# Window attention of a four-layer stack: VectorE in the loop's order, the routing in fixed slots, exponentials behind copies, weights loaded first

## The chip, the cores and the metric

The kernel runs on one core of a Trainium2 chip. A core has five engines with a queue of instructions each: TensorE (PE: matmuls and weight loads, PEld), VectorE (DVE), ScalarE (ACT), GpSimd (POOL) and SyncE (SP), which here only issues DMAs. The metric is the device time of one execution in microseconds (us). Before the change the median of three runs is 2851.44 us (2844.81 to 2851.49). One further execution was taken by the hardware profiler.

## The reference

Four layers over a batch of 2 images with 256 channels and 32 x 32 positions, in float32. Layers 0 and 1 are attention over the feature map. Their result is read as 2 x 1024 tokens of 256 values, and the layer that concerns us is the third, layer 2:

```
t = t + window_attention(layernorm(t))        # windows of 64 tokens, shifted by 32, 8 heads of 32
t = t + moe2(layernorm(t))                    # 8 experts, top 2 of a softmax router, GELU, 256 -> 1024 -> 256

window_attention(x):  q, k, v = x @ w_qkv.T + b_qkv
                      sim = q k / sqrt(32) + rel_pos[i - j]; masked in the last window; softmax
                      out = (softmax @ v) @ w_out.T + b_out
moe2(x):              p = softmax(x @ Wr + br); weights of the top two, normalised to sum 1
                      h = gelu((layernorm(x) * ln_g[e] + ln_b[e]) @ W1[e] + b1[e])
                      y = h @ W2[e] + b2[e]; weighted sum of the two experts' y
```

The factors ln_g and ln_b are each expert's own. Layer 3 is an additive attention (tanh of q_i + k_j for every pair of tokens of an image) and a second mixture of 8 experts with hidden size 512.

## The kernel before

The tokens lie in `t`, 16 tiles of 128 tokens; tiles 0 to 7 are image 0, 8 to 15 image 1. `window_attention` (line 778) works a tile a slot: 16 slots and 4 more to drain. In slot i, TensorE is given `value(i)` (ps_va), `scores(i)` (ps_s), `turn(i-2)` (transposes of the probabilities, ps_pt), one part of the next group's q and k (`project`, ps_qk), `sums(i-3)` (ps_av) and `output(i-4)` (ps_wo). Five of these take a tile of the pool ps_mm, which has three buffers; ps_s and ps_av have one each. `normed(b)` makes the normalised and transposed tokens of image b; for image 1 it is taken in pieces in slots 0 to 5.

Within the loop, TensorE and ScalarE follow the order in which the program writes the instructions (`manual_schedule` with these two engines). For VectorE, GpSimd and SP a planner fixes the order when the kernel is built: it takes from the instructions that are ready by its own reckoning the one that was written first. On ScalarE the exponential of slot i (L884) is written before the two copies of the turned probabilities of tile i-2 (L909). The score work of a slot on VectorE is L876 (scale and add the position bias), L882 (row maximum), L883 (subtract), then after the exponential L885 (sum) and L886 (reciprocal); the division is a product on GpSimd (L889, two instructions). The output of a tile goes through VectorE (L935: y = ps_wo + b_out) and GpSimd (L936: t = t + y).

The routing of image 0 (`dispatch(2, 0)`) is a generator: each `next` issues one piece. It is a gate for each half of the image (statistics L1087 and L1088, inverse root L1072 to L1079, norm L1097, transposes ps_tr L1108 with copies L1109, router L1137, logits L1141), the `route` (top two, counts over all tokens, prefix sums, slot numbers, tiles' experts, affine rows; L1205 to L1313), a second norm of the normalised tokens, and for each of the 8 token tiles two scatters by GpSimd (L1161) into the DRAM buffer `slots_in`; `shift` then adds the mixture of the experts' b2 to t (ps_wT L1179, ps_b L1187, L1189). From slot 10 on the loop takes three pieces a slot; what is left is step D20 of the plan that follows.

That plan (`Late.run`, line 1704) merges generators by due times: E20 are the experts of image 0 (23 slot tiles of 128 rows: `inputs` loads xr by SP, `turn` ps_x, `up` ps_h, `down` ps_y), D21 the dispatch of image 1, E21 its experts, C20 and C21 gather and add the results, A0 and A1 are layer 3's additive attention, and so on. What is due before E21 (172) is ordered by the planner on every engine; after that TensorE, ScalarE and VectorE follow the merge. Expert weights are gathered by GpSimd (`fetch`, L1322) into tiles `ew`, which lie in a pool opened only after window attention, as does kT of layer 3. SBUF is a stack of pools: a new pool's first writers wait for the last reader of the pools that lay there.

The constructor of `Late` loads small constants of layers 2 and 3 (SP and ScalarE queues); `window_attention` then loads its own weights behind them, at L793 to L796.

Of the kernel before, what the change touches and what calls it, by code (L numbers as in the profile page):

```python
# [69 lines left out]
class Stack:  # L70
# [707 lines left out]
    def window_attention(self, t, late):  # L778
# [7 lines left out]
        with ExitStack() as ctx:  # L786
# [6 lines left out]
            w_qkv = self.load(w, "w_qkv", "(c p) o -> p c o", p=P)  # L793
            w_out = self.load(w, "wa_w_out", "(c p) o -> p c o", p=P)
            b_qk = self.load(w, "b_qk")
            b_v, b_out = self.load_row(w, "b_v"), self.load_row(w, "wa_b_out")  # L796
# [25 lines left out]
            uT, q, k, v, pT, o = {}, {}, {}, {}, {}, {}  # L822
# [22 lines left out]
            def project(g, part):  # L845
# [11 lines left out]
                if part < CC:  # L857
                    nc.scalar.activation(to, ps, AF.Identity, bias=b_qk[:, part : part + 1])
                else:
                    nc.vector.tensor_scalar(to, ps, b_qk[:, part : part + 1], None, ALU.add)  # L860

            def scores(i):
# [21 lines left out]
                nc.scalar.activation(l, l, AF.Exp)  # L884
# [8 lines left out]
            def value(i):  # L893
# [7 lines left out]
                nc.vector.tensor_tensor(v[i], ps, b_v, ALU.add)  # L901
# [25 lines left out]
            def output(i):  # L927
                x = o.pop(i)
                ps = late.misc([P, C], "ps_wo")
                for c in range(CC):  # L930
                    nc.tensor.matmul(
                        ps, lhsT=x[:, c, :], rhs=w_out[:, c, :], start=(c == 0), stop=(c == CC - 1)
                    )
                y = sb.tile([P, C], F32, name="y")
                nc.vector.tensor_tensor(y, ps, b_out, ALU.add)  # L935
                nc.gpsimd.tensor_tensor(t[:, i, :], t[:, i, :], y, ALU.add)  # L936
# [5 lines left out]
            with tc.manual_schedule(engines={engines.PE, engines.Activation}):  # L942
                for part in range(2 * CC):
                    project(0, part)
                for i in range(NT + 4):
# [3 lines left out]
                    if 2 <= i < NT + 2:  # L949
                        turn(i - 2)  # L950
                    if i + 4 < NT:
                        project(i // 4 + 1, i % 4)
                    if i < 6:
                        next(other, None)
                    if 3 <= i < NT + 3:
                        sums(i - 3)
                    if 4 <= i:
                        output(i - 4)
                    if i >= 10:
                        for _ in range(3):  # L960
                            next(route, None)
# [28 lines left out]
class Late:  # L990
# [3 lines left out]
    def __init__(self, ctx, stack, t):  # L994
# [4 lines left out]
        self.early = ctx.enter_context(tc.tile_pool(name="early_sb", bufs=2))  # L999
        self.made = {}  # L1000
# [3 lines left out]
        tl = lambda name, shape: self.w.tile(shape, F32, name=name)  # L1004
        self.wr = {l: stack.load(self.w, n, "(c p) e -> p c e", p=P) for l, n in ((2, "wr"), (3, "gate_w"))}
# [87 lines left out]
    def scale(self, dst, src, tiles, mv):  # L1093
        nc = self.nc
        rs = self.inverse_root(mv[:, :, 1], 1e-5)
        for k, i in enumerate(tiles):
# [47 lines left out]
    def dispatch(self, *key, done=0):  # L1144
# [3 lines left out]
        n = len(tokens)  # L1148
        for half in range(done, n // 4):
            yield from self.gate(l, b, half)  # L1150
        yield from self.route(key, n)
        u = self.u[key]
        if l == 2:
            yield from self.norm(lambda i: u[:, i, :], lambda i: u[:, i, :], range(n))
        p, shares, slots, rows = self.routes[key]
        nc = self.nc
# [13 lines left out]
        if l == 2:  # L1170
            yield from self.shift(*key)
# [412 lines left out]
    def project(self, b, half):  # L1584

        nc, U, R = self.nc, 32, 4
        if half == 0:
            self.qb[b] = self.sb.tile([P, IT, U], F32, name="qb")
            self.kT[b] = self.sb.tile([P, N], F32, name="kT")
# [114 lines left out]
    def run(self, route):  # L1704
# [5 lines left out]
        self.loaded = [  # L1710
            [self.sb.tile([P, WIDE], F32, name=f"ew{k}", bufs=LANES[2]) for k in range(2)] for _ in range(LANES[2])
        ]
# [5 lines left out]
            "D21": (self.dispatch(2, 1), (), 5, 3.45),  # L1718
            "E21": (self.experts(2, 1), ("D21", "E20"), 172, lambda now: 2.43 if now < 205 else 4.4),
            "C20": (self.collect(2, 0), ("E20",), 172, 2.0),  # L1720
            "A0": (self.additive(0), ("C20",), 211, 4.75),
            "N30": (self.gate(3, 0, 0), ("A0 half",), 420, 6.0),
            "C21": (self.collect(2, 1), ("E21",), 456, 2.0),
# [113 lines left out]
```

## Time and profile before

| | us |
|---|---|
| median of three runs | 2851.44 |
| the profiled execution, whole | 2887.74 |
| its span, first to last instruction | 2886.0 |
| TensorE busy in the span | 2635.3 (91%) |
| VectorE, ScalarE, GpSimd busy | 1944.8, 1815.6, 1235.5 |
| last product of layer 1 ends | 1623.2 |
| first projection of window attention (ps_qk) | 1640.5 |
| score addition of slots 0, 8, 12 starts | 1650.76, 1702.93, 1735.97 |
| first scatter of image 0 starts | 1779.64 |
| first product of the experts of layer 2 (ps_h) | 1810.79 |

In the profile's lines, L852 is line 852 of the kernel; `ps_qk<-uT,sb_w_qkv` names what an instruction writes and reads. A row of the timeline or of the chain begins with its start and its length in us. The chain is the work that ended last, followed backwards: at each step to what released the instruction, or to the one before it on its engine; "issue" is time for which nothing is recorded. Busy times in a stretch are by engine, with the number of instructions in brackets; a fp32 matmul counts as two records. PEclk is the clock that TensorE was granted, as a share of full speed.

### The profile page before, as it was taken

Reading aid. Unit: us, or ns where it says so; the run is one execution under the profiler, and the core shown is the slowest. Engines: PE = TensorE matmul, PEld = TensorE weight load, DVE = VectorE, ACT = ScalarE, POOL = GpSimd, SP = SyncE. Lnnn points to the kernel's source line nnn. Section 1 sums busy time; section 2 is a strip of 40 time slices with the busy share of each in tenths; the row PEclk is TensorE's granted clock in tenths of the full one; section 3 lists DMA queues with packets and bytes.
Section 4 is the critical chain, followed back from the end, with each engine's and each line's share of the span. In section 5 each row is a group of like instructions: output and inputs, shape, how many; then the busy total and the mean of one; then the engine's idle time right before and its main releaser. Section 6 shows DMA issues by size and latency. Waiting matters only on the chain. (4 is left out here: it accounts for less than half of the span.)

```text
span 2886.0 us, 77396 instructions
## 1 busy us (share of the span) xinstructions
PE 2635.3 (91%) x32006; PEld 1643.6 (57%) x32006; DVE 1944.8 (67%) x3642; ACT 1815.6 (63%) x2685; POOL 1235.5 (43%) x1302
## 2 busy tenths in 40 slices
PE   7899999999999998799999686999999988999987
PEld 3455555555555555555555454998666632465676
DVE  5999999999999999478789577633422343134242
ACT  2777777778777777255555231211699878889722
POOL 4877777777777775001111134244111112102242
PEclk9999999999999999899999897999999999899998
DMA  3000000000000000111010100543222001322354
GB/s 133 3 3 3 3 3 3 3 3 3 3 3 3 3 3 3 49 31 28 11 31 9 28 1 30 202 134 99 68 81 76 16 24 35 128 67 87 116 166 125
DMA packets 180577, 131.39 MB, mean 46 GB/s; under 512 B 130992, under 2 KB 162368, under 8 KB 173056
## 3 DMA queue, kind: packets, MB, share of 16 engines
q0 software_dynamic: 29232, 81.71, 8.5%
q1 hardware_dynamic: 147824, 44.25, 6.8%
q8 instruction: 251, 4.11, 0.6%
q10 hardware_dynamic: 3168, 0.48, 0.1%
q14 instruction: 102, 0.84, 0.1%
HBM read 181.24 MB, written 29.49 MB: 73 GB/s over the span
## 5 line engine op out<-in xcount | busy, mean ns | idle before, releaser
L188 ACT ACTIVATE sc<-sc,sa_shift 128x1024 f32<-128x1024 f32 x512 | 584.5, 1144 | 153.1 <-DMA sa_shift<-sa_min 150.8
L201 DVE STREAM_TRANSPOSE wt<-sc 128x1024 f32<-128x1024 f32 x512 | 601.5, 1207 | 0.2 <-ACT sc L188 0.2
L1622 ACT ACTIVATE th<-kT,qb 128x1024 f32<-128x1024 f32 x512 | 540.4, 1135 | 66.2 <-PE ps_e L1631 40.1
L211 PEld LDWEIGHTS ps_o<-wt,v 128*64 128x64 f32 x8192 | 444.4, 137 | 188.9 <-issue 106.2
L143 PE MATMUL ps_s<-kT,qT 64*32 64x512 f32 x8192 | 527.6, 595 | 18.0 <-ACT sc L153 17.2
L211 PE MATMUL ps_o<-wt,v 128*64 128x128 f32 x8192 | 505.0, 276 | 26.8 <-DVE oT L372 26.7
L166 POOL TENSOR_TENSOR fold<-sc 128x512 f32<-128x512 f32 x256 | 329.2, 1286 | 195.9 <-ACT sc L153 177.0
L168 POOL TENSOR_TENSOR fold<-sc,fold 128x512 f32<-128x512 f32 x256 | 328.4, 1283 | 21.4
L153 ACT COPY sc<-ps_s 128x1024 f32<-128x1024 f32 x256 | 256.0, 1000 | 111.0 <-PE ps_s L143 57.1
L1631 PE MATMUL ps_e<-th,pick 128*32 128x512 f32 x2048 | 305.7, 613 | 20.5 <-ACT th L1622 9.3
L1404 PEld LDWEIGHTS ps_h<-xe,ew 128*128 128x128 f32 x2320 | 278.1, 194 | 63.6 <-issue 39.0
L150 DVE TENSOR_SCALAR_CACHE_REDUCE sc<-ps_s 128x1024 f32<-128x1024 f32 x256 | 304.3, 1189 | 7.1 <-PE ps_s L143 6.6
L1404 PE MATMUL ps_h<-xe,ew 128*128 128x128 f32 x2320 | 295.0, 281 | 13.7 <-issue 5.6
L1424 PE MATMUL ps_y<-ew,h 128*128 128x256 f32 x1160 | 275.6, 387 | 8.2 <-ACT h L1410 5.6
L143 PEld LDWEIGHTS ps_s<-kT,qT 64*32 64x32 f32 x8192 | 134.4, 106 | 230.2 <-issue 163.4
L1424 PEld LDWEIGHTS ps_y<-ew,h 128*128 128x128 f32 x1160 | 215.6, 193 | 66.7 <-issue 23.0
L630 ACT ACTIVATE sc<-sc,l_least 128x1024 f32<-128x1024 f32 x128 | 146.7, 1147 | 125.8 <-DVE sc L617 125.5
L1415 DVE TENSOR_TENSOR hb<-ps_h,ew 128x512 f32<-128x512 f32 x115 | 79.4, 691 | 207.3 <-PE ps_h L1404 167.1
L1428 DVE COPY y<-ps_y 128x256 f32<-128x256 f32 x99 | 41.9, 423 | 229.7 <-PE ps_y L1424 209.9
L1393 ACT ACTIVATE h<-hb 128x512 f32<-128x512 f32 x115 | 71.5, 623 | 193.0 <-DVE hb L1415 173.7
L636 DVE STREAM_TRANSPOSE wt<-sc 128x1024 f32<-128x1024 f32 x128 | 153.3, 1225 | 46.0 <-ACT sc L630 25.4
L617 DVE TENSOR_SCALAR_CACHE_REDUCE sc<-ps_s 128x1024 f32<-128x1024 f32 x128 | 150.7, 1213 | 40.3 <-PE ps_s L609 40.2
(286 smaller groups left out, 3139.1 us busy)
## 6 DMA issues: line engine op xcount, KB each, us to landing
xr<-slots_in SPq DMA_DIRECT2D x99, 128.0 KB
slots_out<-y SPq DMA_DIRECT2D x99, 128.0 KB
sa_got<-sa_least SPq DMA_DIRECT2D x512, 0.5 KB
sa_shift<-sa_min SPq DMA_DIRECT2D x512, 0.2 KB
slots_in<-zero POOLq DMA_DIRECT2D x46, 128.0 KB
kh<-kh SPq DMA_DIRECT2D x32, 128.0 KB
qh<-qh SPq DMA_DIRECT2D x32, 128.0 KB
sa_sums<-sa_total SPq DMA_DIRECT2D x244, 1.0 KB
```

Source lines behind the costliest of these rows:

```text
L143: nc.tensor.matmul(ps[r][S * c : S * (c + 1), a, :].rearrange("p (b i) -> p b i", i=S), lhsT=qT[half, p, S * i : S * (i + 1)], rhs=keys[ha ...
L150: nc.vector.tensor_scalar(scores[m][0], flat[0], 1.0, None, ALU.mult, ALU.min, accum_out=least[m // 2][:, 0, h : h + 1])
L153: nc.scalar.copy(scores[m][1], flat[1])
L166: nc.gpsimd.tensor_tensor(y, a, b, ALU.subtract)
L168: nc.gpsimd.tensor_tensor(y, a, y, ALU.subtract)
L188: nc.scalar.activation(scores[m][r], scores[m][r], AF.Exp, bias=shift[m // 2][:, r : r + 1], scale=-1.0, accum_out=total[i][:, 2 * p + r, ...
L201: nc.vector.transpose(weights[i, h][:, 2 * p + r, :], x)
L211: nc.tensor.matmul(sums[i][64 * k : 64 * (k + 1)], lhsT=v[:, at % NT, 64 * (at // NT) : 64 * (at // NT + 1)], rhs=weights[i, h][:, :, S * ...
L1404: nc.tensor.matmul(ps[:, j, :], lhsT=a[:, c, at : at + P], rhs=x[:, c, :], start=(c == 0), stop=(c == CC - 1),)
L1424: nc.tensor.matmul(ps, lhsT=h[:, j, :], rhs=w2[:, j, :], start=(j == 0), stop=(j == HB - 1))
L1622: nc.scalar.activation(h, keys, AF.Tanh, bias=self.qb[b][:, s // G, g : g + 1])
L1631: nc.tensor.matmul(pe[i][c * U : (c + 1) * U, a, :], lhsT=self.pick[:, k, :], rhs=h[:, a, :], start=(k == 0), stop=(k == G - 1),)
```

## The change

VectorE joins TensorE and ScalarE in following the written order in the loop. The exponential of a slot (`weigh`) is written behind the copies of tile i-2, and the sum, reciprocal and product (`divide`) behind `sums(i-3)`. The k projections are evacuated by ScalarE, as the q ones; v is copied by ScalarE without its bias. Since each row of probabilities sums to 1, b_v adds b_v @ w_out.T to every output: `output_shift` computes it once with TensorE from a widened copy of b_v and adds it to b_out. GpSimd adds b_out to t ahead of time, and VectorE adds ps_wo to t in one instruction.

The routing pieces come by a table of slots (8: 2, 9: 2, 12 to 18: 4, 6, 6, 4, 3, 3, 2; half of each before the slot's output, half behind), 32 in all, which is the whole dispatch of image 0. The second norm no longer takes statistics: its variance is var * rs * rs of the first norm, and its scaling is done by ScalarE, ahead of the route. The first slot tile's expert weights are fetched before the scatters. `shift` of the two images becomes steps B20 (due 100) and B21 (due 215) of the plan. D21 runs the same changed dispatch.

The weights of window attention are loaded first of all by the constructor of `Late`, into a tile `front` whose halves are later kT of layer 3; the expert weight tiles `ew` move from the later pool to the same early pool.

```diff
-            w_qkv = self.load(w, "w_qkv", "(c p) o -> p c o", p=P)
-            w_out = self.load(w, "wa_w_out", "(c p) o -> p c o", p=P)
-            b_qk = self.load(w, "b_qk")
-            b_v, b_out = self.load_row(w, "b_v"), self.load_row(w, "wa_b_out")
+            w_qkv, w_out, b_qk, b_v, b_out = late.windows
...
-            uT, q, k, v, pT, o = {}, {}, {}, {}, {}, {}
+            uT, q, k, v, pT, o, weights = {}, {}, {}, {}, {}, {}, {}
+            spread = w.tile([P, CC, P], F32, name="spread")
+            nc.gpsimd.tensor_copy(spread, broadcast(b_v, [P, CC, P]))
+            def output_shift():
+                ps = late.misc([P, C], "ps_wo")
+                for c in range(CC):
+                    nc.tensor.matmul(
+                        ps, lhsT=spread[:, c, :], rhs=w_out[:, c, :], start=(c == 0), stop=(c == CC - 1)
+                    )
+                nc.vector.tensor_tensor(b_out, b_out, ps, ALU.add)
...
                 to = (q if part < CC else k)[g][:, part % CC, :]
-                if part < CC:
-                    nc.scalar.activation(to, ps, AF.Identity, bias=b_qk[:, part : part + 1])
-                else:
-                    nc.vector.tensor_scalar(to, ps, b_qk[:, part : part + 1], None, ALU.add)
+                nc.scalar.activation(to, ps, AF.Identity, bias=b_qk[:, part : part + 1])
...
                 nc.vector.tensor_tensor(l, l, broadcast(m, [P, H, WIN]), ALU.subtract)
-                nc.scalar.activation(l, l, AF.Exp)
+                weights[i] = l, m, rec
+            def weigh(i):
+                nc.scalar.activation(weights[i][0], weights[i][0], AF.Exp)
+            def divide(i):
+                l, m, rec = weights.pop(i)
                 nc.vector.tensor_reduce(m, l, AX.X, ALU.add)
...
                     )
-                nc.vector.tensor_tensor(v[i], ps, b_v, ALU.add)
+                nc.scalar.copy(v[i], ps)
...
                     )
-                y = sb.tile([P, C], F32, name="y")
-                nc.vector.tensor_tensor(y, ps, b_out, ALU.add)
-                nc.gpsimd.tensor_tensor(t[:, i, :], t[:, i, :], y, ALU.add)
+                nc.vector.tensor_tensor(t[:, i, :], t[:, i, :], ps, ALU.add)
...
             engines = mybir.EngineType
-            with tc.manual_schedule(engines={engines.PE, engines.Activation}):
+            pieces = {8: 2, 9: 2, 12: 4, 13: 6, 14: 6, 15: 4, 16: 3, 17: 3, 18: 2}
+            with tc.manual_schedule(engines={engines.PE, engines.Activation, engines.DVE}):
                 for part in range(2 * CC):
                     project(0, part)
+                output_shift()
                 for i in range(NT + 4):
...
                         turn(i - 2)
+                    if i < NT:
+                        weigh(i)
                     if i + 4 < NT:
...
                         next(other, None)
+                    if 2 <= i < NT + 2:
+                        nc.gpsimd.tensor_tensor(t[:, i - 2, :], t[:, i - 2, :], b_out, ALU.add)
                     if 3 <= i < NT + 3:
                         sums(i - 3)
+                    if i < NT:
+                        divide(i)
+                    for _ in range(pieces.get(i, 0) // 2):
+                        next(route, None)
                     if 4 <= i:
                         output(i - 4)
-                    if i >= 10:
-                        for _ in range(3):
-                            next(route, None)
+                    for _ in range((pieces.get(i, 0) + 1) // 2):
+                        next(route, None)
             return route
...
         self.early = ctx.enter_context(tc.tile_pool(name="early_sb", bufs=2))
+        self.loaded = [
+            [self.w.tile([P, WIDE], F32, name=f"ew{run}{k}") for k in range(2)] for run in range(LANES[2])
+        ]
         self.made = {}
...
         tl = lambda name, shape: self.w.tile(shape, F32, name=name)
+        self.front = self.w.tile([P, 2 * N], F32, name="front")
+        weights = []
+        for name, cols in (("w_qkv", slice(0, 3 * C * CC)), ("wa_w_out", slice(3 * C * CC, 4 * C * CC))):
+            weights.append(self.front[:, cols].rearrange("p (c o) -> p c o", c=CC))
+            nc.sync.dma_start(out=weights[-1], in_=self.ins[name].rearrange("(c p) o -> p c o", p=P))
+        self.windows = (
+            *weights, stack.load(self.w, "b_qk"), stack.load(self.w, "b_v", "(c p) -> p c", p=P),
+            stack.load_row(self.w, "wa_b_out"),
+        )
         self.wr = {l: stack.load(self.w, n, "(c p) e -> p c e", p=P) for l, n in ((2, "wr"), (3, "gate_w"))}
...
         rs = self.inverse_root(mv[:, :, 1], 1e-5)
+        self.last_norm = mv, rs
         for k, i in enumerate(tiles):
...
         n = len(tokens)
+        nc = self.nc
+        again = self.early.tile([P, n], F32, name="again", bufs=1) if l == 2 else None
         for half in range(done, n // 4):
             yield from self.gate(l, b, half)
-        yield from self.route(key, n)
+            if l == 2:
+                mv, rs = self.last_norm
+                to = again[:, 4 * half : 4 * half + 4]
+                nc.vector.tensor_tensor(to, mv[:, :, 1], rs, ALU.mult)
+                nc.vector.tensor_tensor(to, to, rs, ALU.mult)
         u = self.u[key]
         if l == 2:
-            yield from self.norm(lambda i: u[:, i, :], lambda i: u[:, i, :], range(n))
+            rs = self.inverse_root(again, 1e-5)
+            yield 3.0
+            for i in range(n):
+                nc.scalar.activation(u[:, i, :], u[:, i, :], AF.Identity, scale=rs[:, i : i + 1])
+            yield 5.0
+        yield from self.route(key, n)
         p, shares, slots, rows = self.routes[key]
-        nc = self.nc
+        if key == (2, 0):
+            self.fetch(key, 0)
+            self.fetch(key, 0, 1)
...
             yield None if l == 2 else 0.5
-        if l == 2:
-            yield from self.shift(*key)
...
             self.qb[b] = self.sb.tile([P, IT, U], F32, name="qb")
-            self.kT[b] = self.sb.tile([P, N], F32, name="kT")
+            self.kT[b] = self.front[:, b * N : (b + 1) * N]
         cols = slice(half * CH, (half + 1) * CH)
...
         self.p_x, self.p_h, self.p_y, self.p_e = psum("lt_x", 1), psum("lt_h", 2), psum("lt_y", 1), psum("lt_e", 1)
-        self.loaded = [
-            [self.sb.tile([P, WIDE], F32, name=f"ew{k}", bufs=LANES[2]) for k in range(2)] for _ in range(LANES[2])
-        ]
...
             "D21": (self.dispatch(2, 1), (), 5, 3.45),
+            "B20": (self.shift(2, 0), ("D20",), 100, 5.0),
+            "B21": (self.shift(2, 1), ("D21",), 215, 6.0),
             "E21": (self.experts(2, 1), ("D21", "E20"), 172, lambda now: 2.43 if now < 205 else 4.4),
-            "C20": (self.collect(2, 0), ("E20",), 172, 2.0),
+            "C20": (self.collect(2, 0), ("E20", "B20"), 172, 2.0),
             "A0": (self.additive(0), ("C20",), 211, 4.75),
             "N30": (self.gate(3, 0, 0), ("A0 half",), 420, 6.0),
-            "C21": (self.collect(2, 1), ("E21",), 456, 2.0),
+            "C21": (self.collect(2, 1), ("E21", "B21"), 456, 2.0),
             "A1": (self.additive(1), ("C21", "A0 tanh"), 500, 4.6),
...
             "E30": (self.experts(3, 0, then=(3, 1)), ("D30",), 600, 4.4),
```

## The prediction

> **What bounds the kernel now.** I read the page first (TensorE is busy 91% of a 2886.0 us span; most of the rest of its time lies in a few places), then the busy time in stretches around the changed stage, then the chain that ended last inside it, then the rows of each engine. In the stretches the columns are length, then TensorE, its weight loads, VectorE, ScalarE, GpSimd, then the granted clock and DMA.
>
> ```profile
> 1670.00:1690.00 20.00, 17.82 (x220) 11.28 (x216) 12.60 (x27) 6.43 (x14) 7.68 (x8) 1.00 0.01 2
> 1750.00:1770.00 20.00, 11.94 (x135) 8.42 (x133) 18.17 (x64) 3.88 (x9) 5.63 (x6) 0.76 0.00 1
> 1790.00:1810.00 20.00, 11.28 (x32) 7.15 (x33) 8.95 (x34) 0.00 (x0) 15.95 (x18) 0.50 0.42 152
> 1825.00:1850.00 25.00, 25.00 (x180) 23.66 (x179) 12.76 (x35) 5.06 (x7) 7.26 (x8) 1.00 0.14 38
> ```
>
> Window attention (1640 to 1787) is short of TensorE work in every stretch, the gap up to 1810 more so and at half clock; the experts after it are TensorE without a pause. So time saved before 1810.8 moves everything after it, and TensorE work put after it costs its full length. One step of the loop, from the chain:
>
> ```profile
> 1674.91 0.58 ACT ptT L909
> ...
> 1676.77 1.07 PE ps_wo L931 x4
> 1677.86 0.44 DVE y L935
> ...
> 1678.43 0.73 POOL t L936
> 1679.19 0.43 DVE n_st L1087
> ...
> 1680.03 0.59 DVE l L876
> 1680.64 0.70 DVE wa_m L882
> 1681.36 0.70 DVE l L883
> ...
> 1682.68 0.58 ACT ptT L909
> ```
>
> This is a ring of 7.77 us: the copies of turned probabilities wait behind this slot's exponential, that waits for the score work on VectorE, that stands behind a statistic of the route, and that for GpSimd's addition to t of the output that needed the copies. Entry and exit:
>
> ```profile
> 1635.81 4.57 DMA sb_w_qkv<-in_w_qkv
> 1640.51 8.84 PE ps_qk L852 x16
> ...
> 1779.64 1.20 POOL slots_in L1161
> ...
> 1801.60 2.28 DMA slots_in<-u,rt_slot
> 1804.15 4.49 DMA xr<-slots_in
> ...
> 1810.79 1.28 PE ps_h L1404 x6
> ```
>
> The weights are issued last of SP's list, and sixteen scatters start when the slot numbers exist and end 22 us later.
>
> **The skill.** "SBUF — State Buffer" (SBUF: two separate sides) says that VectorE and GpSimd share one pair of ports as an exclusive lock, so that one blocks for the other's whole instruction. The trace agrees: L883 takes 0.70 us alone and 1.58 at 1656.01 beside a GpSimd product. "TensorE: Matmul & The Clock Gate" (Part 1) says that an idle window of about 3.4 us halves the clock; here eight ps_tr took 2.30 us after 4.95 idle, against 1.04. "ScalarE: Activation LUTs" (Table sets) says that identity is in every table set, so the new scalings load none; the existing Identity at L858 stands beside the exponentials without a load.
>
> **The change, part by part** (times of the profiled execution; l(i) is the start of slot i's score addition, L876).
>
> *Entry.* The weights are issued first, at 1623.3, and land by 1627.9 (4.57). TensorE then waits for its own transposes, over at 1634.3, instead of 1640.5. Sixteen projections 8.84, output_shift 1.07 (priced as ps_wo), ps_va 0.86, ps_s 0.42: l(0) at 1645.5. The bias, last of SP's list with one small load more ahead (0.5), was ready at 1644.7 and is now at 1645.2, just in time. Before: 1650.76. **−5.3**. The other small loads come 2 us later for it (four issues of 0.4 to 0.5); the first of them is used in slot 9. Bounds: 0 if the bias is 5 us late, −6.2 if TensorE alone counts.
>
> *Slots 0 to 7.* VectorE per slot: three score instructions 2.13, wait for the exponential 0.65, sum and reciprocal 0.9, addition to t 0.42: 4.1. The bias of v (0.42), the k copies (0.75) and y leave it; on ScalarE: v copy 0.38, two ptT 1.1, exponential 0.63, projection 0.70, oT 0.38, 3.2 in all. TensorE from start to start at full clock: ps_va 0.96, ps_s 0.42, ps_pt 0.95, ps_qk 1.92, ps_av 0.57, ps_wo 0.97: 5.8. TensorE now bounds, with three ps_mm buffers each freed within 1 to 2 us. The exponential now waits behind the copies; behind it stand the q copy and oT, which TensorE needs only in the next slot. Slots 0 to 3 stay VectorE's, since they carry the second image's inverse root (12 small instructions, 0.20 each, 2.4) and eight norms (0.33 each, 2.7): 5.4, 5.7, 3.8, 3.8. Slots 4 and 5 have a transpose each (0.6) but TensorE is about 1 ahead: 11.8. Slots 6 and 7: 11.6. Sum 42.1: l(8) at 1687.6; before 1702.93. **−15.3** so far.
>
> *Slots 8 to 11, first half of the gate.* VectorE in written order can't fill its waits. Slot 8: 3.7 of its own (4.1 less the addition), four statistics 2.2, addition 0.4, root 2.4, four norms 1.4, one port lock 1.0: 11.1. Slot 9: 3.7, two uT copies 1.35, router 1.7, ps_va and ps_s 1.4, and TensorE, idle 3 us, partly at half clock 1.3: 9.5. Slots 10 and 11: 5.8 each and 0.7 for the clock. Sum 32.9: l(12) at 1720.5; before 1735.97. **−15.5**.
>
> *Slots 12 to 14 up to the slot numbers.* Slot 12: 3.7, 2.2, 0.4 (variance of the normed half), 0.4, 2.4, 1.4, then what the trace shows from the second ps_tr at half clock to the next score (1742.87 to 1751.88) 9.0: 19.5. Slot 13: 3.7, 0.4, root 2.4, eight scalings on ScalarE at 0.3 from start to start 2.4 (an estimate from ACT's 128x256 copies, 0.38 with overlap), exponential 0.3, nine small ones 1.9: 11.1. Slot 14: 3.7, 1.2, counts and copies 1.5, prefix 1.9, addition 0.4, eighteen small ones 3.2: 11.9. Locks 2.0. Sum 44.5: slot numbers at 1765.0, before 1779.6. **−14.6**. Bounds: no locks −18; each piece that crosses engines 2 us dearer, eight of them, +1. The second norm's statistics and scalings left VectorE, which is why this equals the old 43.6 without filling.
>
> *GpSimd.* Before, 21.96 from first to last scatter's start with four additions to t among them. Now fifteen intervals of 1.28 (19.2), two fetches 1.31 each, the last products of probabilities 2.15: 24.0, so the last one starts at 1789.0. From there to the first ps_h it was 9.2 (landing 2.3, xr 4.5, transposes and affine): 1798.2. **−12.6**. The bias additions (0.72) are ready slots earlier. The fetches share the software queue, but the last scatter stands 20 us behind them. SP's xr loads are behind nothing new.
>
> *Experts.* Between 1810.8 and 1990.6 TensorE also did D21's router 1.7, ps_tr 1.0, router 1.7, counts 0.5 and shift (two ps_wT 0.6, four ps_b 1.13: 5.7), 10.6 in all, each at full price. Now shift (2,1) leaves and shift (2,0), which lay in the gap, is planned at 100. But the tokens are final at about 1779 (slot 14 needs 3.1 more, slot 15 its 3.7, then product, turn, ps_av and ps_wo about 7), and the gap lasts to 1798; this part of the plan is ordered by readiness (D21's statistics of u ran at 1811.7 though they are emitted after the route), so gates and some of the shift fill the gap at half clock. Bounds 0 and −10.6; I take **−6**. B21 at 215 falls in a stretch where TensorE is at 25.00 of 25 and ScalarE at 23.5 to 25: **+5.7**, bounds 0 and +8. VectorE's relief in D21 and eight scalings on ScalarE are hidden: 12.8 and 5.1 of 25 busy. The new home of ew and kT costs nothing: same lifetimes, fetched earlier.
>
> Sum −12.6 − 6 + 5.7 = **−12.9**: the profiled 2887.74 becomes 2874.8. That execution is 36.3 above the median of 2851.44; I carry the difference over: **2838.5**.
>
> **Rivals.** (1) *The gap takes nothing*: −12.6 + 5.7 = −6.9, 2844.5. For it: ps_wT ran in sequence at 1937, 60 us after p was ready; against it: TensorE was then full, in the gap it isn't. (2) *Scatters behind the last probabilities* on GpSimd, whose order the planner writes: they wait 3.1 for the rest of slot 14, 3.7 of slot 15, then the product; +6.8 on GpSimd's line, so −6.1, 2845.3. Against it: before, additions to t stand between scatters, so ready work goes first. (3) *VectorE's order becomes the ring*: waits in slots 8 to 14 cost 22 more than counted (1750 to 1770 has VectorE at 18.17 of 20 even with filling, and small instructions of 0.8 to 1.0 beside GpSimd instead of 0.2), about 1.1 for each of twenty pieces: +9, 2860. It decides when l(8) to the slot numbers passes 99 us instead of 77 (before: 76.6). Slower. (4) *The weights don't come early*, the memory being freed with all of layer 1: that is already so at 1623.3, and I count only the list's order.
>
> **Chances.** Likeliest 0.57, own range 2826 to 2843; (1) and (2) together 0.23; (3) 0.20. A measurement here can tell 0.3%, 8.6 us, from no change. Faster 0.58 (a little of (1) included), same 0.22, slower 0.20. The range takes in −27 (no locks, whole gap used: −18 + 2 − 10.6, B21 free) and +11: 2824 to 2862.
>
> **What would show it.** First ps_qk near 1634; slots 4 to 7 at 5.8 with TensorE unbroken and ptT ahead of the exponential; VectorE waiting for ps_tr and router in slots 9 and 12; first scatter near 1765, first ps_h near 1798; ps_wT and routers before that ps_h; ps_b again after C20. Wrong if l(8) comes after 1695, if scatters start after 1775, or if TensorE pauses among the experts.

## The result, and the profile after

| kernel | median, us | n | ratio to before, 95% interval |
|---|---|---|---|
| before | 2848.5 | 20 | |
| changed | 2854.38 | 20 | 1.0018 [1.0012, 1.0024] |

The forecast was 2838.5, counted from 2851.44, the median of three runs; twenty runs of before give 2848.5. The kernel became 5.9 us slower instead. That is less than the 0.3% that I had called no difference, but with twenty runs of each the interval leaves out 1. One thing about the machines has to be known for what follows: the later runs fell on five chips. On three of them the kernel before takes 2848 to 2850, on two 2883 to 2885. Times are therefore compared only as ratios to the kernel before on the same chip, and profiles by stages.

The profile of before that the prediction rests on (2887.74) resembled the second kind. A second one, on a chip of the first kind, took 2847.22, and the pauses of TensorE at 2003 to 2023 and 2445 to 2475 are not in it. It is used below for everything behind the first ps_h.

| | predicted | before | before, 2nd profile | after |
|---|---|---|---|---|
| score addition of slot 0 | 1645.5 | 1650.8 | 1652.5 | 1646.2 |
| of slot 8 | 1687.6 | 1702.9 | 1704.6 | 1692.9 |
| of slot 12 | 1720.5 | 1736.0 | 1737.8 | 1726.5 |
| first scatter | 1765.0 | 1779.6 | 1781.3 | 1772.4 |
| last scatter's start | 1789.0 | 1801.6 | 1803.3 | 1803.3 |
| first ps_h of the experts | 1798.2 | 1810.6 | 1812.9 | 1812.0 |
| first router of layer 3 | | 2285.9 | 2275.5 | 2278.6 |

Of the 15 us promised up to slot 8 ten were there, seven at the first scatter, none at the last one. The same four stretches as before (length, TensorE, its weight loads, VectorE, ScalarE, GpSimd, granted clock, DMA share, GB/s), in the changed kernel:

```profile
1670.00:1690.00 20.00, 20.00 (x230) 12.93 (x232) 12.56 (x22) 10.71 (x23) 7.53 (x8) 1.00 0.01 2
1750.00:1770.00 20.00, 6.95 (x48) 4.89 (x54) 14.76 (x59) 5.65 (x15) 3.17 (x3) 0.59 0.00 1
1790.00:1810.00 20.00, 10.83 (x76) 8.53 (x76) 6.91 (x29) 1.92 (x4) 14.92 (x15) 0.67 0.36 127
1825.00:1850.00 25.00, 25.00 (x182) 23.76 (x181) 9.35 (x21) 6.86 (x12) 6.98 (x7) 1.00 0.24 75
```

The first stretch went from 17.82 to 20.00 on TensorE: the ring of the loop is gone. The second is emptier than before on every engine but ScalarE: VectorE, which should set it, works 14.76 of 20 where it had 18.17. It waits; that it waits because its order is written is shown further down, by the runs with VectorE planned. In the third GpSimd still scatters. In the fourth, among the experts, TensorE has no pause.

The loop in its steady part, from the chain of the changed kernel (start, length, what):

```profile
1675.25 1.02 PE ps_pt L920 x8
1676.27 1.72 PE ps_qk L861 x4
1677.99 0.44 PE ps_tr L849 x4
1678.43 0.57 PE ps_av L929 x16
1679.00 1.06 PE ps_wo L943 x4
1680.06 0.86 PE ps_va L910 x4
1680.92 0.42 PE ps_s L877 x32
1681.34 1.02 PE ps_pt L920 x8
```

TensorE follows itself without a pause, 6.09 us a slot with a transpose, 5.66 without. Before, it was a ring of 7.77 through four engines. The entry, from the same view:

```profile
1640.84 3.08 DMA turned<-in_rel_pos
...
1646.23 0.61 DVE l L882
...
1655.48 5.47 POOL t L971 x8
...
1662.41 1.40 POOL probs L901
1663.85 1.09 PE ps_pt L920 x8
```

The position bias sets slot 0, as estimated, and TensorE's early weights wait for it. Then eight of the new bias additions of GpSimd, which I had put one into each slot, stand in one lump ahead of the second tile's product of probabilities, and ps_pt waits for that.

The exit, GpSimd's row (start, busy, line, what; in brackets the idle time before it and what ended it):

```profile
1772.37 1.12 POOL L1211 DMA_INDIRECT slots_in<-u,rt_slot  x1 [7.60 <-DVE rt_whose L1318]
...
1779.37 1.08 POOL L1211 DMA_INDIRECT slots_in<-u,rt_slot  x1 [0.30 <-DVE rt_affine L1351]
1780.75 1.06 POOL L1370 DMA_INDIRECT ew<-in_l_up,rt_rows  x1 [0.30 <-DVE rt_picked L1350]
1782.11 1.00 POOL L1370 DMA_INDIRECT ew<-in_l_down,rt_rows  x1 [0.31 <-issue]
1783.18 1.03 POOL L901 TENSOR_TENSOR probs<-l,wa_rec 64x512 f32<-64x512 f32 x1
1790.35 1.04 POOL L901 TENSOR_TENSOR probs<-l,wa_rec 64x512 f32<-64x512 f32 x1 [6.14 <-DMA ew<-in_l_down,rt_rows]
...
1803.27 0.97 POOL L1211 DMA_INDIRECT slots_in<-u,rt_slot  x1 [0.30 <-issue]
```

Six scatters, both fetches, one half of the last tile's product, and then a wait of 6.14 until the second fetch has landed. The product reads nothing that was fetched. In the trace its second half waits on eight semaphores (signals that a DMA has landed), one for each of the eight DMAs that GpSimd had issued ahead of it: the six scatters, of which the last landed at 1782.2, and the two fetches. Why the built program has these waits isn't known. The ten scatters left stand behind it, and so does TensorE, which needs the product to end window attention:

```profile
1791.45 1.97 PE L920 MATMUL ps_pt<-ident,probs 128*128 128x128 f32 x8 [10.38 <-POOL probs L901]
```

The chain continues from there:

```profile
1782.11 7.90 DMA ew<-in_l_down,rt_rows
...
1803.27 2.41 DMA slots_in<-u,rt_slot
1805.97 4.59 DMA xr<-slots_in
...
1811.97 3.73 PE ps_h L1452 x18
```

The Trainium skill, "Perfetto Trace Analysis" (DMA Instruction — SWDGE (GPSIMD)), says that such an instruction's end in a profile is the end of writing its descriptors, not of moving the data. The trace agrees: the second fetch has 1.00 in the row and lands 7.90 after its issue.

### The profile page after: what moved, and what is told of

It is laid out like the page before. It is cut to its first block, busy times and chain, and to the rows that moved or that the text cites. A ratio compares the mean times of both kernels' runs of the same rounds, so it can differ in the third digit from the quotient of the medians.

```text
span 2855.4 us, 77379 instructions
## 1 busy us (share of the span) xinstructions
PE 2629.8 (92%) x32010; PEld 1646.6 (58%) x32010; DVE 1929.7 (68%) x3579; ACT 1833.5 (64%) x2725; POOL 1236.7 (43%) x1303
## 5 line engine op out<-in xcount | busy, mean ns | idle before, releaser
L1670 ACT ACTIVATE th<-front,qb 128x1024 f32<-128x1024 f32 x512 | 539.9, 1134 | 54.2 <-PE ps_e L1679 48.2
L1679 PE MATMUL ps_e<-th,pick 128*32 128x512 f32 x2048 | 299.7, 612 | 5.8 <-DVE sc_a L1686 4.4
```

Of the source, the lines that this page charges most:

```text
L1670: nc.scalar.activation(h, keys, AF.Tanh, bias=self.qb[b][:, s // G, g : g + 1])
L1679: nc.tensor.matmul(pe[i][c * U : (c + 1) * U, a, :], lhsT=self.pick[:, k, :], rhs=h[:, a, :], start=(k == 0), stop=(k == G - 1),)
```

## The experiments

**Theory**: the gain is lost on GpSimd behind the slot numbers, by the wait above. **Rivals**: VectorE's written order in slots 8 to 14; TensorE's work moved to where it is full (B20, B21); the lump of bias additions.

### First set: GpSimd's row

The second profile of before:

> The kernel before, unchanged: a second profile of it. The stretches up to E20's end should fall where they did (score additions of slots 0, 8, 12 at 1650.8, 1702.9, 1736.0; first scatter 1779.6; first ps_h 1810.8; last ps_y before E21 joins 1987.0), within 1 us each. Behind that, if the first profile's longer end was its own chance (stalls at 2003 to 2023 and 2445 to 2475), the span is about 2850 and the pauses are absent; if it belongs to the kernel, they come again.

The stretches are as told: 1652.5, 1704.6, 1737.8, 1781.3, 1812.9. All are later by 1.7 to 2.3, where 1 was expected, from the start of the stage on. The span is 2845.5, and the pauses are absent.

Without the early fetches:

```diff
-        if key == (2, 0):
-            self.fetch(key, 0)
-            self.fetch(key, 0, 1)
```

> The changed kernel without its two early weight fetches; the first slot tile's weights are fetched behind the scatters, as before. Theory GpSimd (the gain up to the slot numbers is lost because the last product of probabilities, put among the software DMAs, waits for what was issued ahead of it, the fetch of 7.9 us being the longest): two issues of 1.31 leave the row and the wait of 6.14 shrinks to about the 2.3 of a scatter's landing less a half product, some 1.3: last scatter's start from 1803.3 to 1795, first ps_h from 1812.0 to 1804, time 2846.5. Rival VectorE order (slots 8 to 14 are where the gain goes): the first scatter stays at 1772 and the time stays at 2854 within 2. Rival TensorE (the 5.7 of shift (2,1) behind C20 is the whole loss): 2854 too.

2854.11, ratio 1.0015 [1.0008, 1.0021]. Half of this was right: the last scatter starts at 1795.24. But the first ps_h is at 1810.70 and the time is unchanged. GpSimd's row and TensorE's, in that run:

```profile
1789.90 0.97 POOL L1208 DMA_INDIRECT slots_in<-u,rt_slot  x1 [0.30 <-issue]
1790.94 1.03 POOL L901 TENSOR_TENSOR probs<-l,wa_rec 64x512 f32<-64x512 f32 x1
1792.62 1.04 POOL L901 TENSOR_TENSOR probs<-l,wa_rec 64x512 f32<-64x512 f32 x1 [0.65 <-issue]
...
1795.24 0.97 POOL L1208 DMA_INDIRECT slots_in<-u,rt_slot  x1 [0.31 <-issue]
```

```profile
1799.01 1.99 PE L943 MATMUL ps_wo<-front,oT 128*128 128x256 f32 x8
...
1808.97 0.66 PE L1424 MATMUL ps_x<-ident,xr 128*128 128x128 f32 x2 [5.33 <-DMA xr<-slots_in]
```

The planner now puts the product behind fourteen scatters, so window attention ends at 1801.0. SP issues the first xr at 1801.17, although the last scatter landed at 1797.66. Between them SP waits for TensorE's last ps_wo (what waited, for what, us in total, times, longest):

```profile
SPq L1416 <- PE ps_wo L943: 3.3, 1, 3.3
```

xr lies in a pool that is opened after window attention. That the wait comes from the memory, whose last reader TensorE was, is argued and not shown. The landing of xr then takes 7.8 instead of 4.6, beside four weight fetches. What holds the experts moved from the scatters to the product.

The last product off GpSimd:

```diff
-                    nc.gpsimd.tensor_tensor(
+                    (nc.vector if i == NT - 1 else nc.gpsimd).tensor_tensor(
```

> The changed kernel with both halves of the last tile's product of probabilities on VectorE instead of GpSimd; early fetches stay. Theory GpSimd: no compute stands between software DMAs any more, so nothing waits for the fetch; eighteen issues of 1.3 from 1772.4: last scatter's start 1794.4 in place of 1803.3, first ps_h 1803.5, time 2846. VectorE pays about 1.4, hidden under the scatters. Rivals VectorE order and TensorE: 2854 within 2; if the lane that a fetch holds stops a later scatter instead, the row shows an idle time before a scatter and half of the gain.

2847.23, ratio 0.9997 [0.9989, 1.0005]; first ps_h at 1804.76. GpSimd's row has no wait left:

```profile
1779.59 1.05 POOL L1370 DMA_INDIRECT ew<-in_l_up,rt_rows  x1 [0.30 <-DVE rt_picked L1350]
1780.95 1.08 POOL L1370 DMA_INDIRECT ew<-in_l_down,rt_rows  x1 [0.31 <-issue]
1782.33 1.03 POOL L1211 DMA_INDIRECT slots_in<-u,rt_slot  x1 [0.30 <-issue]
...
1793.89 0.97 POOL L1211 DMA_INDIRECT slots_in<-u,rt_slot  x1 [0.30 <-issue]
```

That is 0.21% less than the changed kernel, some 6 us, and from slot 0's score addition to the first ps_h it is 159.7 against 165.8, 6.1 less. The theory holds for these 6 us. (The first ps_h is 7.2 earlier in the two profiles; 1.1 of that lies ahead of slot 0.)

Without the bias additions:

```diff
-                    if 2 <= i < NT + 2:
-                        nc.gpsimd.tensor_tensor(t[:, i - 2, :], t[:, i - 2, :], b_out, ALU.add)
```

> The changed kernel with the sixteen GpSimd additions of b_out to t left out (b_out, with what b_v gives, is then missing in the output of window attention): the price of their place in a lump at the entry. Theory entry lump: slots 1 and 2 no longer wait for GpSimd, score addition of slot 3 at 1660.5 in place of 1664.4 and of slot 8 at 1688 in place of 1692.9; the first scatter 4 to 5 earlier, at 1767.5, first ps_h 1807.5 with the fetch wait unchanged, time 2849.5. Rival, the lump is covered (slot 8 is set by VectorE's own sum): score addition of slot 8 at 1692 within 1, time 2854.

2854.13, ratio 1.0015 [1.0007, 1.0022]. From slot 0 to slot 8 it takes 45.0 instead of 46.7, to the first ps_h 164.0 instead of 165.8: the lump costs 1.7, not 4 to 5 as expected. With the lump gone, slots 0 to 3 still take 21.5, against the 18.7 that were forecast, so most of that overrun isn't the lump's.

### Second set: the shift of B20, and VectorE's order

```diff
-            "B20": (self.shift(2, 0), ("D20",), 100, 5.0),
+            "B20": (self.shift(2, 0), ("D20",), -11, 0.5),
```

> The changed kernel with step B20 (shift of image 0: two ps_wT of 0.6 and four ps_b of 1.13 on TensorE, 5.7) planned at -11 in pieces 0.5 apart instead of 100, so behind the last ps_wo and ahead of the first experts. Theory shift (the loss behind the first ps_h is that B20 left the gap for the stretch where TensorE is full): first ps_h to layer 3's first router falls from 466.6 to about 463.5, since 5.7 leave and the first gate of D21, 2.7, that filled the gap till now comes back; the first ps_h stays at 1812 within 1, time 2851.5. Rival entry/GpSimd alone (the experts' stretch has nothing to do with it): 466.6 and 2854 stay.

With the product on VectorE as well:

> Both edits: last tile's product on VectorE, and B20 in the gap. If they are independent: 2847.2 less 3 = 2844, ratio to before 0.9980, first ps_h at 1803 to 1805, first ps_h to layer 3's first router 463.5. If they share the gap (it is 8 shorter once the product is off GpSimd, and at half clock B20 takes some 10 of the 13 that are left), first ps_h comes at 1807 and the time is 2846.

And in addition

```diff
-            "B21": (self.shift(2, 1), ("D21",), 215, 6.0),
+            "B21": (self.shift(2, 1), ("D21",), 425, 3.5),
```

> As the one before, and B21 (shift of image 1, the same 5.7) planned at 425 in pieces 3.5 apart instead of 215 in pieces of 6.0, so ahead of C21 in the stretch 2300 to 2400, where TensorE was busy for 92.75 of 100. Theory shift: B21 costs its whole 5.7 at 215 and half of it or less there: 3 to 5 less than the run beside it, 2840. Rival (B21 lies behind ScalarE's tanh, which sets that stretch with 96.6 of 100): no difference, 2844.

These fell on a chip of the second kind (before: 2884.53). Ratios 1.0020 [1.0012, 1.0027], 1.0016 [1.0008, 1.0023] and 1.0024 [1.0014, 1.0033], when the changed kernel, on another chip of that kind, later had 1.0027. B20 put there delays the first ps_h: from slot 0 on it takes 170.6 and 169.2, in the changed kernel on such a chip 168.4. Its products run at half clock (eight records of ps_b 3.77). In the first of these kernels window attention ends at 1799.2, and the gap behind it is too short. In the second it should have ended near 1789, as in the run with the product on VectorE alone; but the last ps_wo ends at 1801.5 there, behind a wait of 8.29 for a copy by ScalarE, and SP issues xr only at 1803.3. The third kernel shows the same (8.95). So these two say little of how well a shift fits into a gap; why the copy came so late is open. B21 at a later date gained nothing. The way to layer 3's first router, 477.6, 473.3 and 471.8, has the chip's pauses in it and decides nothing. These three expectations failed or stayed open; the fourth set takes the shift up again.

The rival in its own run:

```diff
-            with tc.manual_schedule(engines={engines.PE, engines.Activation, engines.DVE}):
+            with tc.manual_schedule(engines={engines.PE, engines.Activation}):
```

> The changed kernel with VectorE taken out of the written order of the loop, so that it is ordered by the planner as before; TensorE and ScalarE stay in written order, all else is as changed. Rival VectorE order (the written order in slots 8 to 14 leaves waits that a planned order would fill): score addition of slot 8 to the first scatter falls from 79.5 to 70 and the time to 2846. My theory: that stretch was near what I had counted (79.5 for 77.4) and the written order is not what loses; 79.5 within 3 and 2854 within 3, or slower where a planned order puts route pieces ahead of scores.

Ratio 0.9987 [0.9978, 0.9996]. Here my theory, that the written order is not what loses, fell and the rival stood: slot 8 to the first scatter took 64.5 in place of 79.5, and the kernel became a little faster than before.

### Third set: beside the control

> The changed kernel, unchanged, as a control beside the next runs: ratio to before 1.0018 within 0.001, first scatter 1772, last scatter's start 1803, first ps_h 1812.

> VectorE out of the written order once more, beside its control: if the written order is the larger loss, ratio to before 0.9987 and to the changed kernel 0.997 (8 to 9 us); score addition of slot 8 to first scatter 64.5 where the control has 79.5, first ps_h about 1805. If the earlier ratio was a matter of that chip, it equals the control within 3 us.

> VectorE planned, and the last tile's product on VectorE: the wait of 3.7 and the products of 2.1 leave GpSimd's row between the scatters: last scatter's start from 1786.2 to 1780.3. Theory GpSimd: first ps_h follows, 1800, ratio 0.997. Rival (first ps_h is held by the gate of D21, whose ps_tr and router run at half clock in the gap, ps_router till 1804): first ps_h stays at 1805 and the ratio at 0.9987.

> As the one before, without the two early fetches: last scatter's start 2.6 earlier, 1777.7; the first weights are issued at 1779 and land 8 later, 1787, before the first ps_h can start. Theory: the early fetch brings nothing once the scatters start at 1758; time as the one before or 1 to 2 less. Rival: the fetches issued right behind the scatters crowd the xr loads (7.8 in place of 4.5 when that was so), and the first ps_h is 3 later.

On one chip (before 2883.16): changed 1.0027 [1.0018, 1.0037]; VectorE planned 0.9992 [0.9983, 1.0000]; with the last product on VectorE 0.9982 [0.9975, 0.9989]; without early fetches 0.9977 [0.9970, 0.9985]. So the written order costs 9.4 us on this chip, and the early fetch brings nothing that can be measured. The two losses don't add up. With VectorE planned, moving the last product brings the first ps_h 3.9 nearer to slot 0 (157.4 in place of 161.3), but the time hardly moves: 0.9992 and 0.9982 here, 0.9962 and 0.9957 on the last chip of the fourth set, each pair with intervals that overlap.

### Fourth set: the shift back in the dispatch

```diff
+        if l == 2:
+            yield from self.shift(*key)
...
-            "B20": (self.shift(2, 0), ("D20",), 100, 5.0),
-            "B21": (self.shift(2, 1), ("D21",), 215, 6.0),
```

> The changed kernel with the shift of both images back in the dispatch, as before (no steps B20 and B21): in the order of TensorE that of image 0 stands behind the last ps_wo and ahead of the first ps_h, that of image 1 among image 0's experts. Theory shift (B20 left the gap for a full TensorE, 4 to 5 behind the first ps_h): first ps_h to layer 3's first router 4 to 5 shorter than the changed kernel's (466.6 on one chip, 477.0 on the other); but the gap is short here and at half clock, so the first ps_h comes 3 later, as in the run with B20 in the gap: ratio 0.0005 to 0.001 under the changed kernel's. Rival (the stretch is longer for another reason, the moved second norm or the chip's own pauses): no difference there, ratio 0.001 higher.

> VectorE planned, last product on VectorE, shift of both images back in the dispatch. The gap is 18 long here (last ps_wo 1779, xr 1797), so image 0's shift, some 10 at half clock, fits and hides: first ps_h stays at 1802 within 2, and the way to layer 3's first router is 4 to 5 shorter than without (474.6): ratio 0.9965 in place of 0.9982. Rival: it pushes D21's gate behind and with it the first ps_h by 3 or more, ratio 0.998.

> The same without the early fetches: TensorE's order has no gate of D21 ahead of the first ps_h, only image 0's shift. First ps_h at 1800 within 2, ratio 0.996 to 0.9975 (0.9977 without the shift put back).

On a chip with before at 2849.0: 1.0028 [1.0013, 1.0042], 0.9925 [0.9912, 0.9938] and 0.9928 [0.9916, 0.9941]. Alone, the shift put back is no gain: from slot 0 to the first ps_h it takes 169.1, 3.3 more than in the changed kernel, which eats the 2.2 that it is shorter behind it. With VectorE planned, the combination beats both kernels, by more than expected. So it was run again beside its neighbours:

> VectorE planned, last product on VectorE, shift back in the dispatch, once more and on one chip with its neighbour: ratio to before 0.9925 where the chip is the one of that run, 0.994 to 0.996 where it is the slower one.

> The same with the shift as steps B20 and B21, as changed (0.9982 on the slower chip). If the shift's place is worth the 4 us that the stretch behind the first ps_h shows, and D21's gate standing ahead of the first ps_x another 4 to 8: 0.4% above its neighbour. If most of the 0.57% between the two earlier runs was the chip: within 0.2% of it.

> VectorE planned and nothing else, on the same chip as these two: 0.1% above the kernel with the last product on VectorE (0.9992 and 0.9982 before); at 0.9987 to 0.9995 of before on either chip.

On one chip (before 2848.42): 0.9931 [0.9915, 0.9947], 0.9957 [0.9943, 0.9970] and 0.9962 [0.9948, 0.9976]. Best: 2826.74. In TensorE's row of that run the gap holds the whole shift of image 0:

```profile
1771.07 0.60 PE L1229 MATMUL ps_wT<-ident,rt_p 128*8 128x128 f32 x4 [0.52 <-DVE t L946]
1772.64 3.41 PE L1237 MATMUL ps_b<-sb_l_b,wT 8*128 8x256 f32 x8 [0.98 <-DVE wT L1231]
1775.99 1.01 PE L1229 MATMUL ps_wT<-ident,rt_p 128*8 128x128 f32 x4
1777.77 3.78 PE L1237 MATMUL ps_b<-sb_l_b,wT 8*128 8x256 f32 x8 [0.77 <-DVE wT L1231]
...
1789.73 0.66 PE L1429 MATMUL ps_x<-ident,xr 128*128 128x128 f32 x2 [7.13 <-DMA xr<-slots_in]
...
1791.32 3.30 PE L1454 MATMUL ps_h<-xe,ew 128*128 128x128 f32 x18
```

It ends 8 us before xr lands; in the changed kernel, with the product late, window attention's own tail lay there. Its neighbour without the shift back is 11.8 slower. Of that the stretch behind the first ps_h shows 4.8. In the two profiles another 6.9 lies ahead of slot 0, which no edit touches, and 6.1 in layer 3, where two profiles of the best kernel differ by as much (below); what the other 7 of the 11.8 are is not settled. VectorE planned alone fell outside its expectation: 0.9962, where 0.9987 to 0.9995 was expected from the two chips of the second kind. Why it is worth more on this chip is open too.

### What the stretch behind the first ps_h obeys

With the prediction's durations (a gate: ps_tr 1.0 and router 1.7; counts 0.5; a shift 5.7), count what a kernel does for the routing on TensorE between the first ps_h and layer 3's first router, and add it to 452.0, which is the second profile of before (462.6) less its own 10.6. Chips of the first kind only:

| kernel | routing work behind the first ps_h | sum | count says | measured |
|---|---|---|---|---|
| before, 2nd profile | router, gate, counts, one shift | 10.6 | (462.6) | 462.6 |
| changed | gate, counts, two shifts | 14.6 | 466.6 | 466.6 |
| last product on VectorE | the same | 14.6 | 466.6 | 467.8 |
| no bias additions | the same | 14.6 | 466.6 | 467.6 |
| no early fetch | router more | 16.3 | 468.3 | 467.5 |
| shift back | two gates, counts, one shift | 11.6 | 463.6 | 464.4 |
| VectorE planned (third) | counts, two shifts | 11.9 | 463.9 | 464.1 |
| its last product on VectorE | the same | 11.9 | 463.9 | 466.9 |
| best without early fetches | two gates, counts, one shift | 11.6 | 463.6 | 465.0 |
| best, twice | most of a router, gate, counts, one shift | 10.4 | 462.4 | 462.8, 462.0 |

All but one lie within 1.4 (the exception shows a clock of 0.96 in 1992 to 2040, where the changed kernel, VectorE planned and the best kernel have 1.00). The sum is an account and not an experiment, and it starts from one profile, so the changed kernel's agreement to a tenth is luck. To within 1.4 it accounts for the changed kernel's end: two shifts and a gate at full price, 4.0 more than before. The run with the shift back points the same way, 2.2 less where the count says 3.0.

### Where the written order lost its time

VectorE in slots 12 to 14, first in the changed kernel:

```profile
1744.65 0.69 DVE L882 SCALAR_TENSOR_TENSOR l<-ps_s,bias 128x512 f32<-128x512 f32 x1 [2.52 <-PE ps_s L877]
...
1749.01 0.98 DVE L1106 TENSOR_SCALAR ir_x<-again 128x8 f32<-128x8 f32 x1
...
1752.76 0.17 DVE L1113 SCALAR_TENSOR_TENSOR ir_y<-ir_a,ir_y 128x8 f32<-128x8 f32 x1
...
1756.44 0.22 DVE L1260 TENSOR_REDUCE rt_one<-rt_lg 128x8 f32<-128x64 f32 x1 [2.12 <-ACT rt_lg L1258]
...
1771.94 0.17 DVE L1314 CAST rt_slot<-rt_one 128x8 uint32<-128x8 f32 x1
```

then with VectorE planned (third run):

```profile
1731.60 0.16 DVE L1106 TENSOR_SCALAR ir_x<-again 128x8 f32<-128x8 f32 x1
...
1736.74 0.17 DVE L1113 SCALAR_TENSOR_TENSOR ir_y<-ir_a,ir_y 128x8 f32<-128x8 f32 x1
1737.64 0.69 DVE L882 SCALAR_TENSOR_TENSOR l<-ps_s,bias 128x512 f32<-128x512 f32 x1 [0.72 <-PE ps_s L877]
...
1745.08 0.21 DVE L1260 TENSOR_REDUCE rt_one<-rt_lg 128x8 f32<-128x64 f32 x1
...
1758.92 0.16 DVE L1314 CAST rt_slot<-rt_one 128x8 uint32<-128x8 f32 x1
```

Written, the inverse root of the second norm stands in slot 13 behind that slot's scores. It runs there from 1749.0 to 1752.9, ScalarE's eight scalings wait for it, the router's exponential for them, and VectorE for that (2.12). Planned, the same root runs in slot 12, while TensorE is at the router and at slot 13's scores, and is done before slot 13 begins. From slot 12's score addition to the slot numbers: 45.6 and 36.4. Slots 8 to 11 gain as well (33.7 and 29.4), and slots 0 to 7 lose a little (46.7 and 47.8).

## Why the prediction was wrong, step by step

- **Entry** (−5.3): right, −4.6 measured (−6.3 from the second profile of before); the bias set it, as said. A single profile is a rough measure here: the other profiles with VectorE in written order have slot 0 from 1643.6 to 1649.6, and no edit of theirs lies ahead of it.
- **Slots 0 to 7** (42.1): 46.7. Slots 4 to 7 are right (5.8 predicted, 5.7 to 6.1 measured). Slots 0 to 3 took 23.2 instead of 18.7. The bias additions, costed at nothing since "ready slots earlier", account for 1.7 of it by the run without them. What is left is 0.5 to 1.0 in each of the four slots, which I undercounted.
- **Slots 8 to 11** (32.9): 33.7, right in sum.
- **Slots 12 to 14** (44.5): 45.6, right. But I took this size as given by the work. Its rival (3) named the mechanism, waits of the written order, and set its threshold at 99 us from slot 8 to the slot numbers; 79.3 were measured, so that branch did not occur as priced. Yet the mechanism was already in the 77 that I counted: planned, the same work took 64.4 to 65.8. I compared written order with before's time, never with the same work planned.
- **GpSimd** (24.0 from the first to the last scatter's start, −12.6 at the first ps_h): this step failed. It measured 30.9: the 6.14 of waiting, and 0.8 in all on the pieces. I counted the two fetches and the last product as issues, and not that a product among the DMAs that GpSimd issues would wait for the transfers. Rival (2) had the product ahead of the scatters and priced that at 6.8. It came among them and cost 6.9, by another wait: the likeness of the two numbers is chance. Moving it off GpSimd gave back 6.1 from slot 0 to the first ps_h.
- **Experts** (−6, then +5.7): the −6 failed. The +5.7 for B21 fits the count; no run tests it by itself. I let gates and shift fill the gap; only the first gate did, since B20 ran at 1917 to 1958, near its planned time. By the count above this stretch is +4.0 instead of −0.3. The gap that was to take the shift was itself taken by the late product: TensorE waits 10.38 for it, until 1791.45, and ends window attention behind it.
- **Sum**: −12.9 plus 13.8 (the first ps_h at 1812.0 instead of 1798.2) plus 4.3 gives +5.2; measured +5.9. The first ps_h is compared with the first profile of before there. With the second, which has it at 1812.9, the sum is +3.1, so 1 to 3 us remain without an account, and the closeness of 5.2 to 5.9 is partly luck.

The conditions that I had named for a wrong forecast: slot 8 after 1695 (it was 1692.9, no), scatters after 1775 (1772.4, no), pauses of TensorE among the experts (it works 177.66 of 178 us from 1812 to 1990, no). The first two watched the stretch that went as told, and the third a stretch that stayed full. What failed lay between them, and in how much work fell into that full stretch.

## What to carry to other kernels

Time saved ahead of a stage is worth what the last engine at its door lets through: list, in order, everything that this engine still has to issue, what each piece waits for, and what is queued behind it. Here a compute instruction on GpSimd between indirect DMAs waited for all of them, so look for such waits, and try that instruction on another engine. And price an order written by hand against the same work in an order that fills waits, not against the kernel before: here the written order of VectorE hid a loss inside a change that otherwise gained. It was 9.4 us beside its control, and some 16 where only ratios from different chips can be compared (1.0018 and 0.9962). With order, last product and shift changed together the kernel takes 0.9925 to 0.9931 of before.

## What the runs showed of the hardware beyond that

Most of the scatters by GpSimd are busy 0.97 and follow each other at 1.28; they land after 2.4, and a weight fetch took 7.90. The Trainium skill, "DMA: Bandwidth & Descriptors" (Bandwidth), has 6.15 of DMA time for 1 MB, about the size of these 128 rows of 2056 values, without the writing of descriptors; here it was 7.90 from issue to landing, and two fetches went out one behind the other, after six scatters.

A short pause can cost TensorE its clock or not. In layer 3 the same products follow the same idle time of 2.11 (in brackets), first in the changed kernel, then in the second profile of before:

```profile
2655.68 1.97 PE L1709 MATMUL ps_pt<-ident,sc_a 128*128 128x128 f32 x8 [2.11 <-ACT sc_a L1697]
2657.58 3.64 PE L1679 MATMUL ps_e<-th,pick 128*32 128x512 f32 x16
```

```profile
2650.28 1.09 PE L1661 MATMUL ps_pt<-ident,sc_a 128*128 128x128 f32 x8 [2.11 <-ACT sc_a L1649]
2651.30 1.92 PE L1631 MATMUL ps_e<-th,pick 128*32 128x512 f32 x16
```

Sixteen records of ps_e take 3.64 and 1.92; the granted clock is 0.5 from 2654.7 to 2661.6 in the first profile and stays at full speed in the second. The Trainium skill, "TensorE: Matmul & The Clock Gate" (Part 1), says that the gate watches a free-running window; then it would matter where in the window the pause falls, which no run here shows. From layer 3's first router to TensorE's last product, two profiles of the best kernel took 569.5 and 562.5. Differences of that size there, in single profiles, say nothing of an edit. And one kernel, unchanged, took 2849 on three chips and 2884 on two.
